# Time-mix and GELU feed-forward layer: the output projection as three float32r passes over truncated operands, and a weight term kept in DRAM

## The chip, the cores and the metric

The kernel runs on one core of one Trainium2 chip. A core has a TensorE (PE, matrix products), a VectorE (DVE), a ScalarE (ACT), a GpSimd (POOL) and a SyncE (SP, which here issues nearly all DMAs), each with its own queue of instructions that it works through in order, and 16 DMA engines. The metric is the device time of one execution in microseconds (us).

## The reference

The input x has 4 sequences of 1024 tokens with 512 channels. It is normalized over the channels, and two branches are added to it: a recurrent time-mix (hidden width 704) and a GELU feed-forward network (hidden width 2048). Cut to what matters:

```python
def _L0_attn_ref(x, ...):
    xx = jnp.concatenate([x[:, 1:2, :], x[:, :-1, :]], axis=1) - x
    k = jnp.einsum('btc,hc->bth', x + xx * time_mix_k, Wk)
    r = jnp.einsum('btc,hc->bth', x + xx * time_mix_r, Wr)
    w = jnp.exp(-jnp.exp(time_decay))
    # for each token t: state = state * w + relu(k_t); out_t = state * r_t
    out = jnp.einsum('bth,ch->btc', out, Wv)
    # layer norm of out over the channels, times ln_gamma, plus ln_beta

def _L0_ffn_ref(x, W0, bias0, W1, bias1):
    X = x.reshape(-1, H).astype(jnp.float16)
    D = jnp.dot(X.astype(jnp.float32), W0.T) + bias0
    D = jax.nn.gelu(D, approximate=False).astype(jnp.float16)
    E = jnp.dot(D.astype(jnp.float32), W1.T) + bias1
    return E.astype(jnp.float16).reshape(B, L, H)

xn = _layernorm(x, axis=-1)
x = x + _L0_attn_ref(xn, ...) + _L0_ffn_ref(xn, ...)
```

The product with Wv is called the output projection below.

## The kernel before

The 4096 tokens are worked through in eight blocks i = 0 to 7 of 512 tokens, two blocks a sequence. Channels and hidden units lie on the 128 partitions: 512 channels are four groups c, the 704 hidden units five groups h of 128 and a half group of 64, and the 2048 units of the feed-forward network 16 chunks n. Output tiles s are 128 tokens by 512 channels, four a block.

**The loop.** A block is 16 iterations, one for each chunk n. In each, TensorE first makes `up` for the chunk two ahead (eight matmuls with the two terms of W0, `w0h` and `w0l`, into the bank `pd`, L659), then `down` for chunk n (eight matmuls that add to four banks `pe`, L681), and then one piece of the time-mix branch. Pieces of chunks 0 to 4 are the five k products of this block, 5 and 6 the half group, 7 to 11 the five r products, and 12 to 15 the output projection of the tiles s = 0 to 3 (in the last block, two at chunk 12 and two at chunk 13). What follows a piece, its evictions above all, is emitted in the next iteration behind the next `up`. The order of TensorE and SP is written out by hand in all blocks; that of VectorE and ScalarE by hand in block 0 alone, and by a scheduler later, which fills in by priority and readiness.

**Arithmetic.** [...]Where a float32 product is wanted in float32r, `three_pass` (L534) splits both operands: u is the operand with its low 12 bits masked away, l the rest. `pa` gathers u and l against the two high terms of the weights (eight matmuls), `pb` a third combination (four matmuls, L335), and ScalarE and VectorE put the two together (L546, L547). The k and r products of blocks 1 to 7 are made in this manner. The output projection is not: `out_full` (L588) multiplies the gated states g by Wv in plain float32 (five matmuls of 128x128 by 512, each shown as two records), and `out_halves` (L600) adds the half group for a pair of tiles with four 64x64 products that lie in the four quadrants of the array.

**What follows the output projection.** `residual` takes the statistics of `po` (L265), normalizes it (L615, L620) and adds it to the residual x (L621). The sum of `pe` is rounded to float16 (`rounded`, L641), added (`finish`, L647) and stored.

**Buffers.** PSUM has eight banks: four for `pe`, four (`ps_mm`) that `pd`, `pa`, `pb`, `ph` and `po` take in turn. A `pd` of the next iteration so takes a bank that an eviction on VectorE or ScalarE has to free. SBUF tiles of 128x512 come from one shared tag q with 53 buffers (`QS`); temporaries have five; w1 has two, kr six. W1 and the split kr weights lie in DRAM as ready-made terms and are loaded for each use; W0's 32 split tiles stay in SBUF.

**The x of the next block** is loaded at chunk 2 (into the same buffer as the residual x, which is loaded at chunk 11), its statistics are taken (L265, L266), POOL makes the reciprocal deviation (L259, L260), VectorE normalizes it (L269) and turns it in 16 transposes (L291). At chunks 11 to 14 it is mixed with its shifted self and split (`mixed`, `split_x`). Block 1 also splits the r weights (`split_kr`) and writes them to DRAM.

Of the kernel before, what the change touches and what calls it, by code (L numbers as in the profile page):

```python
# [22 lines left out]
def time_mix_and_gelu_ffn(  # L23
# [23 lines left out]

    nc = tc.nc  # L50
    B, T, C = x.shape
    HID = wkT.shape[1]
# [3 lines left out]
    NC = C // P  # L56
    NN = N // P
    Q = 32
    QS = 53
    S = 4096.0  # L60
    MASK = -4096

# [19 lines left out]
    def temp(name):  # L82
        return const.tile([P, TB], F32, tag="s", name=name, bufs=5)
# [60 lines left out]
    wv_sb = const.tile([P, NF + 1, C], F32, name="wv_sb")  # L144
    gamma_sb = const.tile([P, C], F32, name="gamma_sb")
    beta_sb = const.tile([P, C], F32, name="beta_sb")
    b1_sb = const.tile([P, C], F32, name="b1_sb")

    def load_late_constants():
        for h in range(NF):  # L150
            nc.sync.dma_start(wv_sb[:, h, :], wvT[h * P : (h + 1) * P, :])
        for half in range(2):
            nc.sync.dma_start(wv_sb[half * HF : (half + 1) * HF, NF, :], wvT[H0:, :])
        nc.sync.dma_start(gamma_sb, gamma.partition_broadcast(P))
        nc.sync.dma_start(beta_sb, beta.partition_broadcast(P))
        nc.sync.dma_start(b1_sb, bias1.partition_broadcast(P))


    def split(hi, lo, raw):
# [1 line left out]
        nc.vector.tensor_sub(lo, raw, hi.bitcast(F32))  # L161

    G = TB // P
    w0 = {}

    w0_raw = {}

# [2 lines left out]
        nc.sync.dma_start(raw, w0T[c * P : (c + 1) * P, g * TB : (g + 1) * TB])  # L170

    def split_w0(g, c):
        w0[c, g] = part(f"w0h_{c}_{g}"), part(f"w0l_{c}_{g}")
        split(*w0[c, g], w0_raw.pop((c, g)))

    w1_dram = [dram.tile([P, 2, C], F32R, name=f"w1d_{n}") for n in range(NN)]
    w1_raw = {}
# [52 lines left out]
    def split_half():  # L230
        u = truncated(raw_half.rearrange("p two c k -> p (two c k)"), "half_u")
        u = u.rearrange("p (two c k) -> p two c k", two=2, c=NC)
        for kind in range(2):
            nc.scalar.copy(half_w[kind][:, :, 0, :], u[:, kind])
            nc.vector.tensor_sub(half_w[kind][:, :, 1, :], raw_half[:, kind], u[:, kind])

    def load_kr(j, kind, h):
        terms = [part(f"kr_{j}_{kind}_{h}_{p}", tag="kr", bufs=6) for p in range(3)]
# [223 lines left out]
            nc.gpsimd.tensor_copy(carry[:hw, h : h + 1], dst[:hw, TB - 1 : TB])  # L462

    def state_tile(j, h):
        gs[j, h] = const.tile([P, TB], F32, tag="g", name=f"g_{j}_{h}", bufs=NF)
        return gs[j, h]

    def gated_half(j, st, r):
        def tokens(ap, odd):
            return ap.rearrange("p (s two t) -> p s two t", two=2, t=P)[:, :, odd, :]  # L470

        ghs[j] = const.tile([P, NS // 2, P], F32, tag="gh", name=f"gh_{j}")
# [18 lines left out]
    def raw_r(j, h):  # L491
        pr = bank(f"pr_{j}_{h}")
        for c in range(NC):
            state["pr"] = product(pr, raw_w[1, h], xrs[j, c], c)

        def after():
            nc.vector.tensor_mul(gs[j, h], gs[j, h], pr)

        return after

# [27 lines left out]
    def three_pass(j, kind, h):  # L528
        xs = xks if kind == 0 else xrs
        w = ks.pop((j, kind, h))  # L530
        pa, pb = bank(f"pa_{j}_{kind}_{h}"), bank(f"pb_{j}_{kind}_{h}")
        for c in range(NC):
            for p in range(2):
                nc.tensor.matmul(  # L534
                    pa,
                    w[p][:, c, :],
                    xs[j, c][p],
                    start=(c == 0 and p == 0),
                    stop=(c == NC - 1 and p == 1),
                )  # L540
        for c in range(NC):
            product(pb, w[2], xs[j, c][2], c)

        def after():
            a, y = temp(f"a_{j}_{kind}_{h}"), temp(f"y_{j}_{kind}_{h}")
            nc.scalar.activation(a, pa, AF.Copy, scale=1.0 + 1.0 / S)  # L546
            nc.vector.scalar_tensor_tensor(y, pb, -1.0 / S, a, ALU.mult, ALU.add)  # L547
            if kind == 0:
                nc.scalar.activation(y, y, AF.Relu)  # L549
                scanned(j, h, P, state_tile(j, h), y)  # L550
            else:
                nc.vector.tensor_mul(gs[j, h], gs[j, h], y)

        return after

# [29 lines left out]
    def out_full(i, s):  # L585
        pos[s] = bank(f"po_{i}_{s}")
        for h in range(NF):
            nc.tensor.matmul(  # L588
                pos[s],
                gs[i, h][:, s * P : (s + 1) * P],  # L590
                wv_sb[:, h, :],
                start=(h == 0),
                stop=False,
            )

    def out_halves(i, pair):
        for s in pair:
            rows = slice(s % 2 * HF, (s % 2 + 1) * HF)
            for t in range(0, P, HF):
                nc.tensor.matmul(  # L600
                    pos[s][t : t + HF],
                    ghs[i][rows, s // 2, t : t + HF],
                    wv_sb[rows, NF, :],
                    start=False,
                    stop=True,
                )

    def residual(i, s):
        po = pos.pop(s)
        mv = small([P, 1, 2], "mv1", f"mvy_{i}_{s}", 4)  # L610
        stats_of(mv, 0, po, f"sty_{i}_{s}")
        rstd = rstd_of(mv[:, :, 1], f"ry_{i}_{s}")
        z = zs[i][:, s, :]
        y = temp(f"o_{i}_{s}")
        nc.vector.scalar_tensor_tensor(  # L615
            y, po, mv[:, 0, 0:1], gamma_sb, ALU.subtract, ALU.mult
        )

        def rest():
            nc.vector.scalar_tensor_tensor(y, y, rstd, beta_sb, ALU.mult, ALU.add)  # L620
            nc.vector.tensor_add(z, z, y)  # L621

        return rest

    def out_piece(i, s):
        out_full(i, s)
        if s % 2 == 0:
            return lambda: None
        pair = (s - 1, s)
        out_halves(i, pair)  # L630

        def after():
            rests = [residual(i, s) for s in pair]
            for rest in rests:
                rest()

        return after
# [16 lines left out]
    def up(i, n):  # L654
        pd = bank(f"pd_{i}_{n}")
        g, k = divmod(n, G)
        for c in range(NC):
            for p in range(2):
                nc.tensor.matmul(  # L659
                    pd,  # L660
                    w0[c, g][p][:, k * P : (k + 1) * P],
                    xf[c],
                    start=(c == 0 and p == 0),
                    stop=(c == NC - 1 and p == 1),
                )
# [76 lines left out]
    for i in range(len(blocks)):  # L742
        with tc.manual_schedule(
# [59 lines left out]
            else:  # L803
# [11 lines left out]
                if j <= LAST:  # L815
# [5 lines left out]
                    put(8, turn, 6, 10)  # L821
                    put(9, turn, 10, 14)
                    put(10, turn, 14, 16)
                mix_at = (11, 12, 13, 14)
            put(11 if j <= LAST else 2, fetch_residual)
            if j <= LAST:
                put(10, x16, j)
# [6 lines left out]
            for n in range(NN):  # L834
                ahead = n + AHEAD
                if ahead == NN and j <= LAST:
                    xf = ffn_input(j)
                nxt = (i, ahead) if ahead < NN else (j, ahead - NN)
                gelu = up(*nxt) if nxt[0] <= LAST else None
                for follow in followers:  # L840
                    follow()
                followers = []
                if gelu:
                    d = gelu()
                if n < NN - tail:
# [80 lines left out]
```

## Time and profile before

| | |
|---|---|
| median of 3 runs | 902.84 us (902.22 to 903.78) |
| profiled execution, whole | 901.21 us |
| profiled execution, span from first to last instruction | 899.4 us |
| TensorE clock granted | 0.996 |
| DMA moved | 165.60 MB, mean 184 GB/s |
| `pe` matmuls (L681) | 1008 records |
| `pd` matmuls (L659) | 1024 records |
| output projection, full groups (L588) | 320 records, 142.2 us busy |
| output projection, half group (L600) | 128 records, 17.4 us busy |
| loads of w1 | 110 of 512 KB, 3.5 us to landing |
| loads of kr | 195 of 256 KB, 4.2 us to landing |
| loads of x | 32 of 256 KB, 5.5 us to landing |

Records of a matmul overlap, so their mean length (0.389 us for float32r, 0.592 us for a float32 record) is longer than the distance at which they follow each other; the chain of waits shows that distance. TensorE's weight loads (PEld) run beside its matmuls. Times in a timeline or a window count from the start of the span.

### The profile page before, as it was taken

How to read it: one execution, taken by the hardware profiler on the slowest of the kernel's cores; microseconds unless marked ns; L12 is line 12 of the kernel's file. 1: busy time of each engine (PE TensorE's matmuls, PEld its weight loads, DVE VectorE, ACT ScalarE, POOL GpSimd, SP SyncE). 2: the span in 40 equal slices, each digit the busy share in tenths (PEclk: the TensorE clock that was granted, in tenths of full speed). 3: DMA queues.
4: the chain of work that ended last, by engine and by line, in shares of the span. 5: the costliest groups of instructions: out<-in, count | busy, mean ns of one | idle time of the engine just before them, and what ended most of it. 6: DMA issues, size and time to landing. Idle time of an engine off the chain costs nothing.

```text
span 899.4 us, 10592 instructions
## 1 busy us (share of the span) xinstructions
PE 886.8 (99%) x3688; PEld 656.7 (73%) x3688; DVE 590.6 (66%) x989; ACT 349.1 (39%) x597; POOL 72.7 (8%) x142
## 2 busy tenths in 40 slices
PE   8999999999999999999999999999999999999996
PEld 8666658876688866888568885788767887588854
DVE  5678885976759558594666955678655776565135
ACT  4855524543234332434323442344323344144320
POOL 1100010100201001000111000010011100000000
PEclk9999999999999999999999999999999999999999
DMA  9569647554285543845448454474535664476621
GB/s 271 210 234 334 225 142 249 183 183 149 101 286 168 177 152 120 291 163 172 139 149 292 146 180 140 160 263 153 173 132 193 226 181 136 141 224 208 192 77 47
DMA packets 77888, 165.60 MB, mean 184 GB/s; under 512 B 9199, under 2 KB 15372, under 8 KB 77836
## 3 DMA queue, kind: packets, MB, share of 16 engines
q1 hardware_dynamic: 77776, 164.92, 55.2%
q8 instruction: 29, 0.48, 0.2%
q14 instruction: 23, 0.19, 0.1%
q10 hardware_dynamic: 60, 0.02, 0.0%
HBM read 140.26 MB, written 24.64 MB: 183 GB/s over the span
## 4 chain that ended last, share of the span: by engine, by line
PE 94%; DVE 4%; issue 1%; DMA 1%; POOL 0%; ACT 0%; SPq 0%; DVEq 0%
PE pd L659 25%; PE pe L681 24%; PE po L588 15%; PE pa L534 13%; PE pb L335 7%; PE ph L562 2%; PE pk L335 2%; PE pr L335 2%; PE po L600 2%; DVE xnT L291 1%; DMA x<-in_L_attn_x 1%; PE idle L353 1%; PE pkr L509 0%; DVE xres L647 0%; DVE stx L265 0%
## 5 line engine op out<-in xcount | busy, mean ns | idle before, releaser
L681 PE MATMUL pe<-w,d 128*128 128x512 f32 x1008 | 249.3, 389 | 0.0
L681 PEld LDWEIGHTS pe<-w,d 128*128 128x128 f32 x1008 | 189.1, 188 | 40.7 <-issue 0.8
L659 PE MATMUL pd<-xf,w0h 128*128 128x512 f32 x512 | 209.3, 409 | 1.4 <-DVE y L547 0.8
L659 PE MATMUL pd<-xf,w0l 128*128 128x512 f32 x512 | 199.7, 390 | 0.0
L669 ACT ACTIVATE d<-pd,late_sb 128x512 f16<-128x512 f32 x128 | 87.7, 685 | 191.7 <-PE pd L659 191.4
L588 PE MATMUL po<-wv_sb,g 128*128 128x512 f32 x320 | 142.2, 592 | 0.0
L547 DVE SCALAR_TENSOR_TENSOR y<-pb,a 128x512 f32<-128x512 f32 x70 | 48.2, 689 | 139.4 <-PE pb L335 124.5
L659 PEld LDWEIGHTS pd<-xf,w0h 128*128 128x128 f32 x512 | 96.1, 188 | 38.9 <-issue 16.5
L659 PEld LDWEIGHTS pd<-xf,w0l 128*128 128x128 f32 x512 | 96.2, 188 | 23.6 <-issue 4.3
L588 PEld LDWEIGHTS po<-wv_sb,g 128*128 128x128 f32 x320 | 60.6, 190 | 64.5 <-issue 62.0
L546 ACT ACTIVATE a<-pa 128x512 f32<-128x512 f32 x70 | 41.8, 597 | 115.0 <-PE pa L534 115.0
L674 ACT CAST d<-d 128x512 fp32r<-128x512 f16 x128 | 79.4, 620 | 3.9
L291 DVE STREAM_TRANSPOSE xnT<-x 32x512 f32<-32x512 f32 x112 | 78.7, 702 | 1.8
L265 DVE BATCH_NORM_STATS2 sty<-po 128x6 f32<-128x512 f32 x32 | 21.9, 684 | 85.9 <-PE po L600 85.9
L534 PE MATMUL pa<-hk,kr 128*128 128x512 f32 x140 | 54.5, 389 | 0.0
L534 PE MATMUL pa<-lk,kr 128*128 128x512 f32 x140 | 54.5, 389 | 0.0
L259 POOL TENSOR_SCALAR ry<-mvy 128x1 f32<-128x1 f32 x32 | 15.2, 476 | 394.6 <-DVE mvy L266 394.6
L534 PE MATMUL pa<-hr,kr 128*128 128x512 f32 x120 | 46.7, 389 | 0.0
L534 PE MATMUL pa<-lr,kr 128*128 128x512 f32 x120 | 46.7, 389 | 0.0
L549 ACT ACTIVATE y<-y 128x512 f32<-128x512 f32 x35 | 22.2, 634 | 61.5 <-DVE y L547 61.5
L246 ACT CAST hk<-uk 128x512 fp32r<-128x512 f32 x28 | 17.4, 620 | 58.3 <-DVE uk L213 58.3
L335 PE MATMUL pb<-mk,kr 128*128 128x512 f32 x140 | 37.4, 389 | 0.0
(133 smaller groups left out, 1039.6 us busy)
## 6 DMA issues: line engine op xcount, KB each, us to landing
w<-w1d SPq DMA_DIRECT2D x110, 512.0 KB, 3.5
kr<-krd SPq DMA_DIRECT2D x195, 256.0 KB, 4.2
x<-in_L_attn_x SPq DMA_DIRECT2D x32, 256.0 KB, 5.5
w1d<-w SPq DMA_DIRECT2D x16, 512.0 KB, 2.9
xres<-in_L_attn_x SPq DMA_DIRECT2D x32, 256.0 KB, 4.6
krd<-wt SPq DMA_DIRECT2D x30, 256.0 KB, 3.6
out<-xres SPq DMA_DIRECT2D x28, 256.0 KB, 4.4
w0raw<-in_L_ffn_W SPq DMA_DIRECT2D x16, 256.0 KB, 5.4
```

The source lines that it names most:

```text
L265: nc.vector.bn_stats(st6, src)
L291: nc.vector.transpose(dst[i * Q : (i + 1) * Q, :, :, j, :], src[j * Q : (j + 1) * Q, :, :, i, :],)
L335: return nc.tensor.matmul(dst, w[:, c, :], src, start=(c == 0), stop=(c == NC - 1))
L534: nc.tensor.matmul(pa, w[p][:, c, :], xs[j, c][p], start=(c == 0 and p == 0), stop=(c == NC - 1 and p == 1),)
L546: nc.scalar.activation(a, pa, AF.Copy, scale=1.0 + 1.0 / S)
L547: nc.vector.scalar_tensor_tensor(y, pb, -1.0 / S, a, ALU.mult, ALU.add)
L549: nc.scalar.activation(y, y, AF.Relu)
L588: nc.tensor.matmul(pos[s], gs[i, h][:, s * P : (s + 1) * P], wv_sb[:, h, :], start=(h == 0), stop=False,)
L659: nc.tensor.matmul(pd, w0[c, g][p][:, k * P : (k + 1) * P], xf[c], start=(c == 0 and p == 0), stop=(c == NC - 1 and p == 1),)
L669: nc.scalar.activation(d16, pd, AF.Gelu, bias=b0_sb[:, n : n + 1])
L674: nc.scalar.copy(d, d16)
L681: nc.tensor.matmul(pe[s] if sum_ is None else sum_, d[:, s * P : (s + 1) * P], w1[p][:, cols], start=(n == first and p == 0), stop=(n == e ...
```

## The change

The output projection of blocks 2 to 7 is made by a new function `out_three_pass`, one tile at a time: 11 float32r matmuls into a bank `oa` and six into a bank `ob`, put together by ScalarE and VectorE, after which `residual` works on the SBUF result in place of PSUM. `gated` splits each g behind its gating multiplication with `split_x` (mask, copy, subtraction, combination), and `gated_half` does so for the half group; its u and l share one tile of 128 partitions, so that `oa` takes them in one matmul over 128 rows, while `ob` takes its combination over 64 rows. Blocks 0 and 1 keep the float32 form. The five and a half groups of Wv are split in block 1 by `split_wv`, at chunks 3, 6, 8, 9, 10 and 11.

To make room, W0's low term leaves SBUF: in block 1 the 16 tiles are written to DRAM (`store_w0l`, four at each of chunks 0, 2, 4 and 6), and from block 2 on a 128x512 tile of it is loaded for each chunk (`load_w0l`), two `up`s ahead, into one of three buffers. Wv and g move to the shared tag q, which has 63 buffers now. In blocks from 2 on the mixing for the next block goes from chunks 11 to 14 to chunks 12 to 15.

```diff
-    QS = 53
+    QS = 63
+    RAW_OUT = 2
...
+    def store_w0l(g):
+        for c in range(NC):
+            terms = w0l[c, g].rearrange("p (n k) -> p n k", k=P)
+            stores.append((w0l_dram[g][:, :, c, :].bitcast(F32), terms.bitcast(F32)))
+
+    def load_w0l(i, n):
+        if i > 1:
+            w0ls[i, n] = part(f"w0l_{i}_{n}", tag="w0l", bufs=3)
+            g, k = divmod(n, G)
+            src = w0l_dram[g][:, k].rearrange("p c k -> p (c k)")
+            nc.sync.dma_start(w0ls[i, n].bitcast(F32), src.bitcast(F32))
...
+    def split_wv(h):
+        raw = wv_raw[h]
+        u = truncated(raw, f"vu_{h}")
+        d = temp(f"vd_{h}")
+        nc.vector.tensor_sub(d, raw, u)
+        if h < NF:
+            wv[h] = [part(f"wv_{h}_{p}") for p in range(3)]
+            nc.scalar.copy(wv[h][0], u)
+            nc.scalar.activation(wv[h][1], d, AF.Copy, scale=S)
+            nc.vector.scalar_tensor_tensor(wv[h][2], d, -S, u, ALU.mult, ALU.add)
+        else:
...
+    def gated(j, h, r):
+        g = gs[j, h]
+        nc.vector.tensor_mul(g, g, r)
+        if j >= RAW_OUT:
+            gs[j, h] = split_x(g, f"g_{j}_{h}")
+
     def gated_half(j, st, r):
+        if j >= RAW_OUT:
+            g = temp(f"gh_{j}")
+            nc.vector.tensor_mul(g[:HF], st[:HF], r)
+            u, l = temp(f"gu_{j}"), temp(f"gl_{j}")
+            nc.vector.tensor_scalar(
+                u[:HF].bitcast(I32), g[:HF].bitcast(I32), MASK, None, ALU.bitwise_and
+            )
+            ghs[j] = part(f"gha_{j}"), part(f"ghb_{j}")
+            nc.scalar.copy(ghs[j][0][:HF], u[:HF])
+            nc.vector.tensor_sub(l[:HF], g[:HF], u[:HF])
+            nc.scalar.copy(ghs[j][0][HF:], l[:HF])
+            nc.vector.scalar_tensor_tensor(
+                ghs[j][1][:HF], l[:HF], -S, u[:HF], ALU.mult, ALU.add
+            )
+            return
...
-        y = temp(f"o_{i}_{s}")
+        y = temp(f"o_{i}_{s}") if i < RAW_OUT else po
...
+    def out_three_pass(i, s):
+        cols = slice(s * P, (s + 1) * P)
+        pa, pb = bank(f"oa_{i}_{s}"), bank(f"ob_{i}_{s}")
+        for h in range(NF):
+            for p in range(2):
+                nc.tensor.matmul(
+                    pa, gs[i, h][p][:, cols], wv[h][p], start=(h == 0 and p == 0), stop=False
+                )
+        nc.tensor.matmul(pa, ghs[i][0][:, cols], wv[NF][0], start=False, stop=True)
+        for h in range(NF):
+            nc.tensor.matmul(pb, gs[i, h][2][:, cols], wv[h][2], start=(h == 0), stop=False)
+        nc.tensor.matmul(
+            pb, ghs[i][1][:HF, cols], wv[NF][1][:HF], start=False, stop=True
+        )
+
+        def after():
+            a, y = temp(f"oa_{i}_{s}"), temp(f"oy_{i}_{s}")
+            nc.scalar.activation(a, pa, AF.Copy, scale=1.0 + 1.0 / S)
+            nc.vector.scalar_tensor_tensor(y, pb, -1.0 / S, a, ALU.mult, ALU.add)
+            residual(i, s, y)()
+
+        return after
...
+        cols = slice(k * P, (k + 1) * P)
+        low = w0ls.pop((i, n)) if i > 1 else None
+        for c in range(NC):
+            wl = w0l[c, g][:, cols] if i < 2 else low[:, c * P : (c + 1) * P]
+            for p, w in enumerate((w0h[c, g][:, cols], wl)):
...
-                mix_at = (11, 12, 13, 14)
+                mix_at = (11, 12, 13, 14) if i < RAW_OUT else (12, 13, 14, 15)
+            if i == 1:
+                for g in range(NN // G):
+                    put(2 * g, store_w0l, g)
+                for h, n in enumerate((3, 6, 8, 9, 10, 11)):
+                    put(n, split_wv, h)
...
+                two_on = (i, ahead + 2) if ahead + 2 < NN else (j, ahead + 2 - NN)
+                if two_on[0] <= LAST:
+                    load_w0l(*two_on)
```

More of the change, by code (lines that the diff above doesn't have):

```diff
@@ L143, in time_mix_and_gelu_ffn @@
     raw_half = part("raw_half", F32).rearrange("p (two c k) -> p two c k", two=2, c=NC)
-    wv_sb = const.tile([P, NF + 1, C], F32, name="wv_sb")
     gamma_sb = const.tile([P, C], F32, name="gamma_sb")
@@ L147, in time_mix_and_gelu_ffn @@
     b1_sb = const.tile([P, C], F32, name="b1_sb")
+    wv_raw, wv = {}, {}
     def load_late_constants():
+        for h in range(NF + 1):
+            wv_raw[h] = part(f"wvraw_{h}", F32)
         for h in range(NF):
-            nc.sync.dma_start(wv_sb[:, h, :], wvT[h * P : (h + 1) * P, :])
+            nc.sync.dma_start(wv_raw[h], wvT[h * P : (h + 1) * P, :])
         for half in range(2):
-            nc.sync.dma_start(wv_sb[half * HF : (half + 1) * HF, NF, :], wvT[H0:, :])
+            nc.sync.dma_start(wv_raw[NF][half * HF : (half + 1) * HF], wvT[H0:, :])
         nc.sync.dma_start(gamma_sb, gamma.partition_broadcast(P))
@@ L163, in time_mix_and_gelu_ffn @@
     G = TB // P
-    w0 = {}
+    w0h, w0l, w0ls = {}, {}, {}
+    w0l_dram = [dram.tile([P, G, NC, P], F32R, name=f"w0d_{g}") for g in range(NN // G)]
     w0_raw = {}
@@ L172, in split_w0 @@
     def split_w0(g, c):
-        w0[c, g] = part(f"w0h_{c}_{g}"), part(f"w0l_{c}_{g}")
-        split(*w0[c, g], w0_raw.pop((c, g)))
+        w0h[c, g], w0l[c, g] = part(f"w0h_{c}_{g}"), part(f"w0l_{c}_{g}")
+        split(w0h[c, g], w0l[c, g], w0_raw.pop((c, g)))
+    def store_w0l(g):
[8 more added lines that the diff above has]
+            nc.sync.dma_start(w0ls[i, n].bitcast(F32), src.bitcast(F32))
     w1_dram = [dram.tile([P, 2, C], F32R, name=f"w1d_{n}") for n in range(NN)]
@@ L235, in split_half @@
             nc.vector.tensor_sub(half_w[kind][:, :, 1, :], raw_half[:, kind], u[:, kind])
+    def split_wv(h):
[9 more added lines that the diff above has]
+        else:
+            wv[h] = [part(f"wv_{h}_{p}") for p in range(2)]
+            nc.scalar.copy(wv[h][0][:HF], u[:HF])
+            nc.scalar.activation(wv[h][0][HF:], d[HF:], AF.Copy, scale=S)
+            nc.vector.scalar_tensor_tensor(
+                wv[h][1][:HF], d[:HF], -S, u[:HF], ALU.mult, ALU.add
+            )
     def load_kr(j, kind, h):
@@ L464, in state_tile @@
     def state_tile(j, h):
-        gs[j, h] = const.tile([P, TB], F32, tag="g", name=f"g_{j}_{h}", bufs=NF)
+        gs[j, h] = part(f"g_{j}_{h}", F32)
         return gs[j, h]
-    def gated_half(j, st, r):
+    def gated(j, h, r):
[3 more added lines that the diff above has]
+            gs[j, h] = split_x(g, f"g_{j}_{h}")
+    def gated_half(j, st, r):
+        if j >= RAW_OUT:
[9 more added lines that the diff above has]
+            nc.scalar.copy(ghs[j][0][HF:], l[:HF])
+            nc.vector.scalar_tensor_tensor(
+                ghs[j][1][:HF], l[:HF], -S, u[:HF], ALU.mult, ALU.add
+            )
+            return
         def tokens(ap, odd):
             return ap.rearrange("p (s two t) -> p s two t", two=2, t=P)[:, :, odd, :]
-        ghs[j] = const.tile([P, NS // 2, P], F32, tag="gh", name=f"gh_{j}")
+        ghs[j] = part(f"gh_{j}", F32)[:, : NS // 2 * P]
+        ghs[j] = ghs[j].rearrange("p (s t) -> p s t", t=P)
         for odd in range(2):
@@ L496, in after @@
         def after():
-            nc.vector.tensor_mul(gs[j, h], gs[j, h], pr)
+            gated(j, h, pr)
         return after
@@ L551, in after @@
             else:
-                nc.vector.tensor_mul(gs[j, h], gs[j, h], y)
+                gated(j, h, y)
         return after
@@ L590, in out_full @@
                 gs[i, h][:, s * P : (s + 1) * P],
-                wv_sb[:, h, :],
+                wv_raw[h],
                 start=(h == 0),
@@ L602, in out_halves @@
                     ghs[i][rows, s // 2, t : t + HF],
-                    wv_sb[rows, NF, :],
+                    wv_raw[NF][rows],
                     start=False,
@@ L606, in out_halves, with residual @@
                 )
-    def residual(i, s):
-        po = pos.pop(s)
+    def residual(i, s, po):
         mv = small([P, 1, 2], "mv1", f"mvy_{i}_{s}", 4)
@@ L623, in residual @@
         return rest
+    def out_three_pass(i, s):
[11 more added lines that the diff above has]
+            pb, ghs[i][1][:HF, cols], wv[NF][1][:HF], start=False, stop=True
+        )
+        def after():
[4 more added lines that the diff above has]
+        return after
     def out_piece(i, s):
+        if i >= RAW_OUT:
+            return out_three_pass(i, s)
         out_full(i, s)
@@ L632, in after @@
         def after():
-            rests = [residual(i, s) for s in pair]
+            rests = [residual(i, s, pos.pop(s)) for s in pair]
             for rest in rests:
@@ L656, in up @@
         g, k = divmod(n, G)
+        cols = slice(k * P, (k + 1) * P)
+        low = w0ls.pop((i, n)) if i > 1 else None
         for c in range(NC):
-            for p in range(2):
+            wl = w0l[c, g][:, cols] if i < 2 else low[:, c * P : (c + 1) * P]
+            for p, w in enumerate((w0h[c, g][:, cols], wl)):
                 nc.tensor.matmul(
                     pd,
-                    w0[c, g][p][:, k * P : (k + 1) * P],
+                    w,
                     xf[c],
```

## The prediction

> **What bounds the kernel now.** I read the page's first two parts first, then the waits of the TensorE, then the chain of waits in one block's output projection, then stage windows, then VectorE's timeline.
>
> ```profile
> PE 886.8 (99%) x3688; PEld 656.7 (73%) x3688; DVE 590.6 (66%) x989; ACT 349.1 (39%) x597; POOL 72.7 (8%) x142
> PEclk9999999999999999999999999999999999999999
> ...
> PE pd L659 <- DVE y L547: 0.8, 1, 0.8
> PE pd L659 <- DVE y L573: 0.6, 1, 0.6
> ...
> 436.40 1.82 PE pe L681 x8
> 438.22 4.29 PE po L588 x10
> 442.51 1.02 PE po L600 x8
> 443.53 2.04 PE pd L659 x8
> 445.57 1.81 PE pe L681 x8
> ...
> 357.73:364.08 6.35, 6.35 (x29) 5.26 (x29) 3.08 (x4) 2.54 (x4) 0.00 (x0) 1.00 0.86 272
> 364.08:370.42 6.34, 6.34 (x29) 5.25 (x29) 3.50 (x5) 2.98 (x5) 0.00 (x0) 1.00 0.87 302
> 370.42:376.77 6.35, 6.35 (x30) 5.26 (x29) 2.31 (x3) 2.54 (x4) 0.00 (x0) 1.00 0.87 296
> ...
> 383.23 1.92 DVE L269 TENSOR_SCALAR x<-x,mvx,rx 128x512 f32<-128x512 f32 x4 [0.29 <-POOL rx L260]
> 399.22 0.68 DVE L573 TENSOR_TENSOR y<-ph,a 64x512 f32<-64x512 f32 x1
> 405.38 0.68 DVE L547 SCALAR_TENSOR_TENSOR y<-pb,a 128x512 f32<-128x512 f32 x1
> ```
>
> TensorE is busy 99% at full clock and waits for data 1.4 us in its own row: its instruction stream is the time. A set of eight float32r matmuls costs 1.81 us (0.227 each), five full float32 ones (ten records, two each) 4.29 us (0.858 each). The windows give busy PE, PEld, DVE, ACT, POOL, then clock, DMA share and GB/s for chunks 0 to 2 of block 3: the DMA engines stand at 0.86 to 0.87 there. The last lines are two PSUM evictions that come close to being late (below).
>
> **What the Trainium skill says.** "TensorEngine Tiling (Array Packing)", Key Properties: a change of tiling mode, not just of tile, drains TensorE. The trace agrees: after 64x64 work the next eight matmuls take 2.04 us instead of 1.81. "TensorE: Matmul & The Clock Gate", Why this matters for your kernels: a single matmul over fewer rows takes as long as over 128. No row of before shows one alone in float32r; I use 0.227 for it. "VectorE: DVE Perf Modes", The TRN2 errata: a float32 tensor_tensor of N columns takes (N+151)/0.96 ns, 691 for 512; the trace has 684 to 691, so new DVE operations of these kinds are priced by existing rows.
>
> **The change part by part.**
>
> *TensorE.* Before, two token tiles cost 4.29 + 4.29 + 1.02, and the switch costs the following sets 0.03 and 0.23: 9.86 us. After, each tile has 10 + 1 matmuls into one bank and 5 + 1 into another: 17 x 0.227 = 3.86, or 7.71 a pair. That would be 2.15 less for each of 12 pairs (blocks 2 to 7): 25.8 us.
> The last of the 17 contracts over 64 rows, so the array goes into a 64x128 tiling and back, once per token tile, 24 times. Price: the old 64x64 set should take 2 x 0.429 = 0.86 if its four quadrants run side by side; it took 1.02, and the set behind it 0.23 too long: 0.39 a round trip. Row tiling alone may be cheaper, and a float32r matmul has the same tail (record 0.389, pitch 0.227: 0.16 to drain on either side). Bounds 0 and 0.5; I take 0.35, 8.4 us in all. Net TensorE gain 25.8 - 8.4 = 17.4 us.
>
> *VectorE, blocks 2 to 6, chunks 3 to 8.* The built order moves the statistics of the next x: before, the fourth aggregate came ahead of the scan and of two splits; after, it stands behind the scan, with only one 0.67 us split between it and the normalization. The chain in before: x arrives (376.43), the aggregate runs at 380.35, POOL's rstd (0.64 + 1.85) ends 2.7 us behind it, and the normalization starts at 383.23, having waited 0.29. After, adding the starts of the reordered items, the aggregate stands 5.8 us behind the arrival instead of 3.9, the normalization 1.9 later, and everything up to the second half eviction (L573) with it. That eviction started at 399.22 and ended 0.68 later; the bank it frees is taken by the pd set that started at 401.25, so about 1.25 us were to spare: 0.6 us late. From there the new half product (0.68 + 0.42 + 0.68 + 0.69 = 2.47 for two gh of 0.42) runs among transposes ahead of the pb eviction (405.38 before, needed for the pd at 407.60): 0.2 us more.
> x can arrive later as well. Chunks 0 to 2 carry 256 KB more each. At 0.87 for 302 GB/s the ceiling is about 350 GB/s (an estimate); three chunks need 290 + 40 = 330. That leaves x late by 0 to 2 us; I take 0.6. In all 0.8 + 0.6 = 1.4 a block, 7 us for five. Bounds 0 and 3.
>
> *VectorE, chunks 7 to 15.* Each of five g gets mask 0.42, subtraction 0.69, combination 0.69: chunk 7 to 11 goes from 1.4 to 3.2 us of the 6.35 (the windows had DVE nearly idle there). Chunks 12 to 15 get an extra eviction of 0.69: mixing 4.0 and residual 3.7 give 7.7 us, about 7.2 by the start-to-start distances of the timeline, against a chunk of 3.63 + 3.86 + 0.35 = 7.8. It just fits: cost nothing, hidden by TensorE; without the switch cost it would be about level. The four e16 that free pe for block j end some 10 us after the third piece, and down needs them at 10.7 to 11.0. ScalarE at 39% has room for the 0.6 us copies.
>
> *Block 1.* Six splits of Wv (mask, subtraction, combination: 1.8 us each, and two ACT copies) go where DVE already stalled PE (both PE waits above are here). The built order puts the first into a 2.6 us idle wait for x and moves four transposes behind the y eviction. Following the two orders side by side, the half eviction comes about 2.3 us late, later ones 1.7 to 2.9. The 16 stores of W0's low terms (256 KB in 512-byte pieces) run in chunks 0 to 6 and crowd x and w1. I take 3 us; bounds 0 and 8.
>
> *SP and W0's low term.* Each chunk issues one 256 KB load behind w1 (0.32 us of issue), 96 in all, 25 MB. It has a buffer of its own (three), so it waits for nothing but its turn; it leaves some 9 us before its up and kr loads of this size land in 4.2. Behind it on SP are kr, x and w1; none gains a wait on compute. Nothing, unless the DMA engines saturate (rival C).
>
> *End.* Before, DVE runs 12.6 us from the last pair's statistics (884.08) to the last add (896.64). After, the third tile's residual runs a piece earlier, and behind the last piece stand one residual with its eviction (0.69 + 0.67 + 0.18 + 0.74 + 0.74 + 0.68 = 3.7), two bases (1.3), the adds of two whole tiles (2.6) and of four half tiles (3.3): 10.9. Gain about 1.5.
>
> **Sum.** Profiled execution 901.2 - 17.4 + 7 + 3 - 1.5 = 892.3. The median of the runs shown stands 1.6 above the profiled execution (902.84 against 901.21), so 894.
>
> **Rivals.**
> A, the forecast: less TensorE work, a drain for every 64-row matmul, DVE lateness in chunk 8. 887 to 900. Chance 0.52.
> B, the plain count: tiling by rows costs next to nothing and the stalls are small. For it: the trace of before has no 64x128 form at full clock, and splitting columns, not rows, may be what cost the 0.39. Against: the page above, which names any change of mode. 901.2 - 25.8 - 1.5 + 2 to 8 = 876 to 882, 877 to 884 as a median: about 881. Chance 0.22.
> C, slower: x lands late because the DMA engines, at 0.87 in chunks 0 to 2 of each block, are pushed to their ceiling. For it: block needs of about 330 GB/s against some 350, and x stands last in that queue. Against: the fill before chunk 0 and after chunk 4 (0.30 share) is low, so the backlog clears. Each us of lateness is a us of stall in blocks 1 to 6. It decides from where six blocks lose 17.4 + 1.5, some 3.2 us a block, so x later by about 2.5. At 4 us: 901.2 - 18.9 + 6 x 4.8 = 911, 913 as a median. Chance 0.16.
> D, no difference: gain and stalls cancel within 1.8 us. Chance 0.10.
>
> **How the numbers follow.** A measurement of this kernel can tell about 0.2% (1.8 us) from no change. A and B are faster: 0.74. D is the same: 0.10. C is slower: 0.16. The predicted time is A's, 894. The range leaves out the fast part of B and most of C: 880 to 904; A's own is 887 to 900.
>
> **What would show it.** Right: the output matmuls in 3.9 to 4.4 us a tile; the pd set behind them over 1.9; PE waits for DVE evictions (half and pb) of about 1 us once a block in blocks 2 to 6 near chunk 8; POOL's rx named for 2 us before the normalization; DVE near 76% of its span (590.6 and about 91 more). Wrong: a pd set of 1.81 behind the 64-row matmul (B), or pd waiting for w0l, or DVE for x by over 4 us (C). The most doubtful steps are the 0.35 and the lateness of x.

## The result, and the profile after

The kernel after takes 891.75 us (median of 4 runs, 891.38 to 892.05) against 902.53 us for the kernel before in the same comparison: ratio 0.9878, 95% interval 0.9861 to 0.9895. Its profiled execution took 891.54 us, with a span of 889.7, 9.7 less than before.

The first part of the page of the kernel after (busy time, share of the span, instructions), then rows of its waits (engine and line, what it waited for, us in total, times, longest):

```profile
PE 874.0 (98%) x3760; PEld 683.6 (77%) x3760; DVE 676.6 (76%) x1133; ACT 389.5 (44%) x675; POOL 75.5 (8%) x142
```

```profile
PEld ob L697 <- issue: 8.4, 24, 0.4
...
PEld pd L748 <- DVE y L635: 6.9, 6, 2.0
PEld pd L748 <- DVE y L609: 5.5, 8, 0.8
PE pd L748 <- DVE y L635: 4.4, 5, 1.6
...
PE pd L748 <- DVE y L609: 1.9, 6, 0.4
```

The line numbers have moved: L748 is the `pd` set, L770 the `pe` set, L635 the half eviction, L609 the pb eviction, L691 to L697 the new output projection. TensorE still sets the time, but now waits for VectorE some 6 us in its own row. The first of these rows names nothing that it waits for: it is the weight load of the 64-row matmul, idle 0.35 us each of 24 times. The chain of waits of the kernel after in block 3 (start, us, what) shows what stands there:

```profile
438.54 2.27 PE oa L691 x10
440.81 0.23 PE oa L694
441.04 1.13 PE ob L696 x5
442.17 0.43 PE ob L697
442.60 2.01 PE pd L748 x8
444.61 1.81 PE pe L770 x8
```

Sixteen matmuls at 0.227 us, then one that takes 0.43, then a `pd` set of 2.01 instead of 1.81: one trip into the 64-row form and back costs 0.40 us beside the matmul itself.

Where the 9.7 us went can be read from the starts of the `pd` sets, one for each chunk. The four output chunks of a block and the one behind them took 7.52 + 9.47 + 7.65 + 9.47 + 6.48 = 40.59 us before and 7.78 + 3 x 7.88 + 6.45 = 37.87 after.

| | predicted, us | measured, us |
|---|---|---|
| output projection, six blocks at 2.72 less | -17.4 | -16.3 |
| stalls in chunks 7 to 9, blocks 2 to 6 | +7 | +8.8 |
| block 1 | +3 | -0.3 |
| end, behind the last output piece | -1.5 | -1.6 |
| start and block 0 | 0 | -0.2 |

The start also differs from one execution to the next: the first `pd` set begins 32.8 us into the span in the two executions compared here, and 33.0 to 34.5 in those of the experiments, none of which changes anything ahead of it. Their spans are therefore read by chunks below.

The stalls are the second row of interest. Chunk 7 is 5.2 us longer over five blocks than before, chunk 8 2.9, chunk 9 0.7. VectorE's timeline of the kernel after in block 4 (start, us, instruction, idle time before it and what ended it), where chunk 3 began at 477.43:

```profile
483.79 0.70 DVE L304 BATCH_NORM_STATS2 stx<-x 128x6 f32<-128x512 f32 x1 [3.47 <-DMA x<-in_L_attn_x]
...
489.29 0.17 DVE L305 BATCH_NORM_AGGREGATE mvx<-stx 128x2 f32<-128x6 f32 x1
...
491.35 1.91 DVE L308 TENSOR_SCALAR x<-x,mvx,rx 128x512 f32<-128x512 f32 x4 [1.25 <-POOL rx L299]
...
507.50 0.68 DVE L635 TENSOR_TENSOR y<-ph,a 64x512 f32<-64x512 f32 x1
...
508.95 0.68 DVE L516 TENSOR_TENSOR gh<-st,y 64x512 f32<-64x512 f32 x1
...
513.02 0.68 DVE L525 SCALAR_TENSOR_TENSOR ghb<-gl,gu 64x512 fp32r<-64x512 f32 x1
...
514.45 0.69 DVE L609 SCALAR_TENSOR_TENSOR y<-pb,a 128x512 f32<-128x512 f32 x1
```

Three distances tell the story: from the start of chunk 3 to the first statistics of x (6.36 here), from there to the second half eviction (23.71), and from that to the pb eviction (6.95). Between the second and the last of these lines only the 1.25 us for POOL is idle: from the arrival of x on, VectorE works through a queue. The `pd` set of chunk 8 is due 29.92 us behind the start of chunk 3, and its bank is free 0.74 us after the half eviction starts, so this one must start by 29.18; the pb eviction, due for chunk 9's `pd` at 36.27, by 35.53. In block 3 of the kernel before, chunk 3 began at 371.17, x arrived with this line, and the two evictions started at 399.22 and 405.38:

```profile
376.43 0.69 DVE L265 BATCH_NORM_STATS2 stx<-x 128x6 f32<-128x512 f32 x1 [2.32 <-DMA x<-in_L_attn_x]
```

The means over blocks 2 to 6, in us:

| | x behind chunk 3 | x to half eviction | half to pb eviction | stalls, chunks 7 / 8 / 9 (sum of five) |
|---|---|---|---|---|
| before | 5.67 | 22.96 | 6.01 | 0.1 / 0.1 / 0.0 |
| after | 6.47 | 23.77 | 6.95 | 5.3 / 3.1 / 0.7 |

So each of three distances grew by 0.8 to 0.95 us, and there were only 0.55 to spare on the mean. x itself lands later in fuller windows. The stage windows of chunks 2 and 3 of block 4 (busy PE, PEld, DVE, ACT, POOL, then clock, DMA share, GB/s), first in the kernel before, then in the kernel after:

```profile
473.40:479.75 6.35, 6.35 (x29) 5.25 (x28) 3.44 (x5) 2.98 (x5) 0.56 (x1) 1.00 0.89 316
479.75:486.10 6.35, 6.35 (x29) 5.26 (x28) 2.16 (x3) 2.54 (x4) 0.19 (x1) 1.00 0.81 268
```

```profile
471.09:477.43 6.34, 6.34 (x29) 5.26 (x28) 3.52 (x5) 2.98 (x5) 0.56 (x1) 1.00 0.99 332
477.43:483.78 6.35, 6.35 (x29) 5.26 (x28) 1.92 (x2) 2.54 (x4) 0.18 (x1) 1.00 0.93 313
```

### The profile page after: what moved, and what is told of

The parts are those of the page before. It is cut to its first block, busy times and chain, and to the rows that moved or that the text cites. A ratio compares the mean times of both kernels' runs of the same rounds, so it can differ in the third digit from the quotient of the medians.

```text
span 889.7 us, 11084 instructions
## 1 busy us (share of the span) xinstructions
PE 874.0 (98%) x3760; PEld 683.6 (77%) x3760; DVE 676.6 (76%) x1133; ACT 389.5 (44%) x675; POOL 75.5 (8%) x142
## 4 chain that ended last, share of the span: by engine, by line
PE 55%; DVE 19%; DMA 3%; issue 2%; POOL 1%; ACT 0%; SPq 0%; DVEq 0%
PE pd L748 15%; PE pe L770 14%; PE pa L596 9%; DVE xnT L330 6%; PE oa L691 6%; PE pb L374 4%; DMA x<-in_L_attn_x 3%; PE ob L696 3%; PE po L650 2%; DVE stx L304 1%; DVE g L492 1%; DVE y L609 1%; PE ob L697 1%; DVE lr L286 1%; DVE y L635 1%
## 5 line engine op out<-in xcount | busy, mean ns | idle before, releaser
L770 PE MATMUL pe<-w,d 128*128 128x512 f32 x1008 | 249.0, 390 | 0.0
L770 PEld LDWEIGHTS pe<-w,d 128*128 128x128 f32 x1008 | 189.2, 188 | 39.6 <-issue 0.2
L748 PE MATMUL pd<-xf,w0h 128*128 128x512 f32 x512 | 207.7, 406 | 6.5 <-DVE y L635 4.4
L748 PE MATMUL pd<-xf,w0l 128*128 128x512 f32 x512 | 199.8, 390 | 0.0
L748 PEld LDWEIGHTS pd<-xf,w0h 128*128 128x128 f32 x512 | 96.1, 188 | 42.3 <-issue 10.3
L609 DVE SCALAR_TENSOR_TENSOR y<-pb,a 128x512 f32<-128x512 f32 x70 | 48.2, 689 | 94.0 <-PE pb L374 83.1
L748 PEld LDWEIGHTS pd<-xf,w0l 128*128 128x128 f32 x512 | 96.3, 188 | 20.6 <-issue 1.9
L691 PE MATMUL oa<-wv,hg 128*128 128x512 f32 x120 | 46.9, 391 | 0.0
L691 PE MATMUL oa<-wv,lg 128*128 128x512 f32 x120 | 46.7, 389 | 0.0
L285 ACT CAST hk<-uk 128x512 fp32r<-128x512 f32 x28 | 17.4, 622 | 47.5 <-DVE uk L234 47.5
L650 PE MATMUL po<-wvraw,g 128*128 128x512 f32 x80 | 35.6, 592 | 0.0
```

Of the source, the lines that this page charges most:

```text
L650: nc.tensor.matmul(pos[s], gs[i, h][:, s * P : (s + 1) * P], wv_raw[h], start=(h == 0), stop=False,)
L691: nc.tensor.matmul(pa, gs[i, h][p][:, cols], wv[h][p], start=(h == 0 and p == 0), stop=False)
L748: nc.tensor.matmul(pd, w, xf[c], start=(c == 0 and p == 0), stop=(c == NC - 1 and p == 1),)
L770: nc.tensor.matmul(pe[s] if sum_ is None else sum_, d[:, s * P : (s + 1) * P], w1[p][:, cols], start=(n == first and p == 0), stop=(n == e ...
```

## The experiments

**The price of the 64-row matmul.** Rows of zeros let the last matmul of `ob` run over all 128 rows.

```diff
+            nc.gpsimd.memset(wv[h][1][HF:].bitcast(F32), 0.0)
...
-            ghs[j] = part(f"gha_{j}"), part(f"ghb_{j}")
+            if not ghb:
+                ghb.append(part("ghb"))
+                nc.gpsimd.memset(ghb[0][HF:].bitcast(F32), 0.0)
+            ghs[j] = part(f"gha_{j}"), ghb[0]
...
-            pb, ghs[i][1][:HF, cols], wv[NF][1][:HF], start=False, stop=True
+            pb, ghs[i][1][:, cols], wv[NF][1], start=False, stop=True
```

> The half group's combination and its weights get 64 rows of zeros each, written once, and the last matmul into ob runs over 128 rows; nothing else is changed. Theory (the change of tiling mode costs 0.41 us a tile, 24 times): the pd set behind it falls from 2.01 to 1.81 us and the piece from 4.06 to 3.86; 9.8 us less than the kernel after, less what VectorE cannot follow in chunks 12 to 15: 881 to 885. Rival (the set is long for another reason, such as the bank it waits for): pd stays at 2.01 and the time at 891 to 892.

Measured: 883.53 us (882.35 to 885.46), ratio to before 0.9796 (0.9783 to 0.9809). The chain of waits of this kernel, same block and columns as above:

```profile
437.54 2.27 PE oa L696 x10
439.81 0.23 PE oa L699
440.04 1.13 PE ob L701 x5
441.17 0.23 PE ob L702
441.40 1.81 PE pd L753 x8
```

The same 17 matmuls, 0.43 down to 0.23 and 2.01 to 1.81, and the output chunks are 7.48 us in place of 7.88. VectorE, busy 6.7 to 7.2 us in such a chunk of block 4, keeps up. The stalls of chunks 7 to 9 stay (8.5 us in all). That the change of form, and not the bank, costs the time is shown.

The opposite check leaves that matmul out altogether.

```diff
-            nc.tensor.matmul(pb, gs[i, h][2][:, cols], wv[h][2], start=(h == 0), stop=False)
-        nc.tensor.matmul(
-            pb, ghs[i][1][:HF, cols], wv[NF][1][:HF], start=False, stop=True
-        )
+            nc.tensor.matmul(
+                pb, gs[i, h][2][:, cols], wv[h][2], start=(h == 0), stop=(h == NF - 1)
+            )
```

> The last matmul into ob, over 64 rows, is left out, and with it the half group's third term; everything else is as in the kernel after. Theory (what the change of mode costs is 0.41 us beside the 0.227 of the matmul): each of the 24 tiles is shorter by 0.64, chunks 12 to 15 take 7.26 us, and the time falls by 14 to 15.5 us to 876 to 878. Rival (VectorE, busy 6.9 us in each of these chunks, sets their length once TensorE needs less than about 7.5): chunks of 7.4 to 7.5 and 881 to 883.

Measured: 879.23 us (878.83 to 880.88), ratio 0.9749 (0.9736 to 0.9762). The output chunks took 7.25 us as the theory has it, so VectorE does not set them. The time lies between the two forecasts for other reasons, as far as the profiled execution shows them (880.88 us, the slowest of the four): the stalls of chunks 7 to 9 were 10.5 us instead of 9.0, 3.7 of them in block 5, where the half eviction came 24.55 us behind an x that was itself late (6.62); the first `pd` set began 1.4 us later; and from chunk 3 of block 7 to the end only 1.5 us were gained, where four tiles at 0.63 would give 2.5.

**When x arrives.** At chunk 2, x is issued ahead of kr.

```diff
+                    if k == 4 and j <= LAST:
+                        put(2, fetch_x)
                     if k > 1:
                         put(k - 2 + 2 * (k > 6), fetch_kr, i, kind, h)
...
-                    put(2, fetch_x)
```

> At chunk 2 the load of the next x is issued ahead of the kr loads instead of behind them. Theory (the stalls of 8.7 us in chunks 7 to 9 come from a VectorE chain that begins with the arrival of x): x lands 1.5 to 2.7 us earlier, the half eviction with it, the stalls fall to 0 to 3 us, and the time to 884 to 887. Rival 1 (the new work behind the half eviction is what stalls, whenever x comes): 891 to 892. Rival 2 (kr is late now, and the k product waits for it): PE waits for kr, 892 to 900.

Measured: 884.59 us (883.37 to 885.44), ratio 0.9805 (0.9792 to 0.9817). In block 4, whose chunk 3 starts at 476.04, SP's timeline now has

```profile
474.85 1.75 SPq L105 DMA_DIRECT2D x<-in_L_attn_x  x4
476.70 1.91 SPq L279 DMA_DIRECT2D kr<-krd  x3
```

while x's issue came 0.57 us behind that start in the kernel after. The statistics of x begin 4.32 us behind it on the mean, 2.15 earlier; the half eviction follows 24.40 behind x, 0.6 more than without the edit; the stalls of chunks 7 to 9 are 1.5 us in place of 9.0. Nothing waits for kr. So the lateness is one chain that begins with x, as the first theory has it.

**What makes x late.** Four loads of W0's low term around x's are left out.

```diff
-        if i > 1:
+        if i > 1 and n in (3, 4, 5, 6):
+            w0ls[i, n] = w0ls[i, n - 1]
+        elif i > 1:
```

> From block 2 on, the four loads of W0's low term that lie around the load of x (for the chunks 3 to 6) are left out and the tile of the chunk before them is used again, so that the feed-forward output of these chunks lacks its right low term; the number of matmuls is the same. Theory (these transfers make x late by the 0.8 us that the kernels before and after differ in, on the mean of blocks 2 to 6): x's statistics start 5.5 to 5.8 us behind the chunk's boundary again instead of 6.5, the stall in chunk 7 falls by 0.6 to 0.8 us a block, chunk 8 keeps its 0.6, and the time is 887 to 889. Rival (x is late for SP's issue or another reason, or the order of the statistics alone makes the stall): 891 to 892.

Measured: 890.84 us (889.07 to 892.47), ratio 0.9874 (0.9861 to 0.9887), not told apart from the kernel after. The first half of the theory holds: x's statistics begin 5.70 us behind the boundary, as before the change (5.67). Of the second half, some holds: chunk 7 stalls 3.3 us in five blocks instead of 5.3, where 3 to 4 us less were forecast. The profiled execution as a whole does not show these 2.0 us: its first `pd` set began 1.4 us later, and block 1, which the edit leaves as it is, took 0.8 us more behind an x that came 6.49 us behind the boundary instead of 5.70. VectorE's timeline in block 4 of this kernel, chunk 3 starting at 478.32:

```profile
484.97 0.69 DVE L306 BATCH_NORM_STATS2 stx<-x 128x6 f32<-128x512 f32 x1 [3.76 <-DMA x<-in_L_attn_x]
...
490.54 0.55 DVE L310 TENSOR_SCALAR x<-x,mvx,rx 128x512 f32<-128x512 f32 x1 [1.48 <-POOL rx L301]
...
509.02 0.68 DVE L637 TENSOR_TENSOR y<-ph,a 64x512 f32<-64x512 f32 x1
```

The scheduler has reordered the queue as well: the normalization starts 5.57 us behind x instead of 7.56, yet the half eviction comes 24.05 behind it instead of 23.71. The normalization's place does not matter; the work and the idle time in front of the eviction do, and the wait for POOL grew from 1.25 to 1.48. So the half eviction gains 0.4 us on the mean where x gains 0.8. Blocks also differ by chance: x came 5.08 to 6.65 behind.

**The order of the statistics.**

```diff
-                    put(4, stats, *range(NS))
+                    put(3, stats, *range(NS))
```

> The statistics of the next x get their priority at chunk 3 instead of 4, which puts the fourth aggregate ahead of the scan again, as in the kernel before. Theory (the order of the aggregate and the scan delays the normalization by some 0.8 to 1.9 us a block): the stall in chunk 7 falls by 0.8 us in each of five blocks, the time to 885 to 889. Rival (only the arrival of x counts): the time stays at 891 to 892. If the statistics block VectorE while x is on its way, slower: 893 to 897.

Measured: 890.45 us (889.91 to 891.75), ratio 0.9873 (0.986 to 0.9885): not told apart from the kernel after. In four of five blocks the half eviction came 23.3 to 23.5 us behind x, 0.35 less than after, with the wait for POOL at 0.94; the fifth took 24.5, with 1.06 us of idle time for a later part of x. In this profiled execution chunk 7 stalls 2.7 us instead of 5.3, but three quarters of that come from an x that arrived 0.4 us earlier, which the edit does not touch. The theory overstated it: the order is worth 0.35 us a block in four blocks and 0.13 on the mean.

**The memory half of the change alone.** All blocks project in float32.

```diff
-    RAW_OUT = 2
+    RAW_OUT = 8
```

> All eight blocks keep the output projection in plain float32; the splits of Wv and W0's low term in DRAM with its load for every chunk stay. This is the memory half of the change alone. Theory: W0's low term costs no wait of its own but makes x late by about 1 us, and the scheduler's order delays the normalization, so chunk 7 stalls by 0.8 us in five blocks, and without the new half product chunk 8 does not: 905 to 908. Rival 1 (the loads are free and all stalls come from the new half product): as before, 902 to 903. Rival 2 (the loads cost more than the pieces after show, hidden by the shorter output pieces): 910 or more.

Measured: 907.02 us (906.17 to 909.27), ratio 1.0059 (1.0047 to 1.0071). Its waits:

```profile
PEld pd L748 <- DVE y L635: 5.7, 6, 1.5
PE pd L748 <- DVE y L635: 3.1, 6, 1.1
```

So W0's low term in DRAM and the order that comes with it cost 5 us by themselves: x 6.15 us behind the boundary, the half eviction 23.78 behind x as in the kernel after, and 3.8 us of stall in chunk 7. But the pb eviction follows 6.01 behind the half eviction, as before the change, and chunk 8 stalls 0.7 us in all instead of 3.1. The two halves of the stall are thus parted: chunk 7's is that of x and the order, chunk 8's is that of the new half product (gh, gu, gl, ghb). No `pd` waited for the tile of W0 itself.

**Is VectorE's queue what holds the half eviction?** Ten transposes are left out from block 2 on.

```diff
-                    put(6, turn, 0, 2)
-                    put(7, turn, 2, 6)
-                    put(8, turn, 6, 10)
+                    if i < RAW_OUT:
+                        put(6, turn, 0, 2)
+                        put(7, turn, 2, 6)
+                        put(8, turn, 6, 10)
```

> The kernel after without 10 of the 16 transposes of the next x from block 2 on (the transposed x keeps old values there, so blocks 3 to 7 are computed from partly old input); everything else is left as it is, and VectorE's order has 6 transposes ahead of the second half eviction where it had 10, and none between it and the pb eviction where it had 5 to 6. Theory (from the arrival of x on VectorE is simply full, and the eviction is late by the work that stands in front of it): the second half eviction starts 20.7 to 21.1 us behind x's statistics instead of 23.7 to 23.9, and all 8.7 us of stall in chunks 7 to 9 of blocks 2 to 6 go: 882 to 884. Rival 1 (the eviction waits for TensorE or ScalarE, whatever VectorE has to do): 891 to 892. Rival 2 (only the half product's own chain is late, in chunk 8): 887 to 889.

Measured: 886.9 us (886.49 to 888.48), ratio 0.983 (0.9816 to 0.9843), none of the forecasts' mechanisms alone. VectorE's and ScalarE's timelines of this kernel in block 4, chunk 3 starting at 476.86 and x's statistics at 483.00:

```profile
503.25 0.71 DVE L330 STREAM_TRANSPOSE xnT<-x 32x512 f32<-32x512 f32 x1
506.30 0.68 DVE L635 TENSOR_TENSOR y<-ph,a 64x512 f32<-64x512 f32 x1 [2.33 <-ACT a L634]
```

```profile
504.00 1.66 ACT L343 CAST x<-xnT 128x512 f16<-128x512 f32 x3 [1.45 <-DVE xnT L330]
505.68 0.58 ACT L634 COPY a<-ph 64x512 f32<-64x512 f32 x1
```

VectorE was free at 503.97, 20.97 us behind x, as the theory has it. But with fewer transposes the float16 copies of x are ready sooner, the order has three of them ahead of the eviction's first half on ScalarE, and they wait for the last transpose. The half eviction so waits 2.33 us for ScalarE and comes at 23.3, and chunk 7 stalls 3.3 us. In chunk 8, where the transposes between the two evictions are gone, these lie 3.88 us apart and 0.7 us of stall is left. The queue is confirmed for chunk 8; in chunk 7 the edit moved a second queue, so it does not settle the matter there. That an eviction is late by what stands ahead of it on its engines is all that it shows.

**Block 1.** The first split of Wv is moved from chunk 3 to chunk 7.

```diff
-                for h, n in enumerate((3, 6, 8, 9, 10, 11)):
+                for h, n in enumerate((7, 6, 8, 9, 10, 11)):
```

> The kernel after with one change: the first split of Wv goes from chunk 3 of block 1 to chunk 7, so that it no longer lies in VectorE's wait for x but between the two half evictions. Theory (this wait is what hid it, and the prediction's 3 us for block 1 fell away for such reasons): the second half eviction comes 1.8 us later than 29.3 behind the boundary, block 1 is 1.5 to 1.8 us longer than 110.5, the time 893 to 894. Rival (other idle time of VectorE takes it up): block 1 at 110.5 to 110.8, the time 891.5 to 892.

Measured: 892.66 us (891.54 to 894.24), ratio 0.9897 (0.9881 to 0.9913). The expectation misplaced the split: it came to lie behind the second half eviction, which kept its place, 29.17 us behind chunk 3 (29.31 in the kernel after). Block 1 took 111.0 us, 0.5 more. That alone would show little, since runs that leave block 1 as it is take 110.45 to 111.3 by when x comes. But its chunks 8 to 11 take 27.1 to 27.2 us in all of those, and 27.8 here: 0.6 more. Two thirds of the split's 1.8 us were absorbed. So the wait for x hides some of it, not the 1.5 us or more that I expected.

**Both helpful edits together**, with zeros and x first:

> The two edits that helped alone, in one kernel: 64 rows of zeros for the last matmul into ob, and x loaded ahead of kr. They act in different chunks (12 to 15, and 2 to 9), so theory: their gains add, 8.2 and 7.2 us off the 891.75 of the kernel after, 875 to 878. Rival (the shorter chunks 12 to 15 bring the transfers of the next block closer together, or VectorE is full there): 879 to 883.

Measured: 875.9 us (875.41 to 877.05), ratio 0.9712 (0.9699 to 0.9726). The gains add: output chunks of 7.48 us, stalls of 0.4 us in chunks 7 to 9.

**Block 1 in three passes too**, on top of these:

```diff
-    RAW_OUT = 2
+    RAW_OUT = 1
```

> The kernel with both edits, and block 1 in three passes too, so that only block 0 is in plain float32; block 1 now splits Wv and g in the same chunks. TensorE needs 34.1 - 30.0 = 4.1 us less in block 1's chunks 12 to 15. Theory (VectorE already makes TensorE wait about 2 us in block 1's chunks 7 to 11, and gets 10 us more there): 2 to 4 us of the gain are lost again, 0 to 2 us less than the kernel with both edits, 874 to 877. Rival (the new work fits between the evictions): 871 to 873. If the splits make chunk 12 wait for wv, slower than the kernel with both edits: 878 to 882.

Measured: 873.31 us (873.21 to 875.17), ratio 0.9685 (0.9672 to 0.9698), 2.6 us less, between theory and rival. In its profiled execution TensorE's 4.1 us are there, block 1's stalls in chunks 7 to 11 grow by 1.9 us (3.6 for 1.7), and chunk 12 is 1.1 too long; the splits of Wv and g do take back most of the gain.

Then the splits of Wv go ahead of x:

```diff
-                for h, n in enumerate((3, 6, 8, 9, 10, 11)):
+                for h, n in enumerate((0, 1, 1, 2, 2, 3)):
```

> The kernel in three passes from block 1 on, with the six splits of Wv at chunks 0, 1, 1, 2, 2 and 3 of block 1 instead of 3, 6, 8, 9, 10 and 11. Theory (VectorE has no room from the arrival of x to the last pb eviction, but idles for 3 us a chunk before it; so the half eviction lies a fixed 23 to 24 us behind x's arrival, plus the work put between): with five splits of 1.8 us ahead of x, the stalls of block 1's chunks 8 to 12, 4.6 us, fall to 0.5 to 2, and the time to 869.5 to 872. Rival (the stalls there come from splitting g, or from evictions waiting for TensorE): 873 to 874. Should the splits run into the pb evictions of chunks 0 to 2, slower: 875 or more.

Measured: 872.79 us (871.77 to 874.9), ratio 0.968 (0.9664 to 0.9697), not told apart. The stalls of chunks 7 to 11 did fall, from 3.6 to 0.9 us. But chunk 4 became 8.47 us long. TensorE's and ScalarE's timelines there:

```profile
168.38 0.50 PE L753 MATMUL pd<-xf,w0h 128*128 128x512 f32 x1 [1.97 <-ACT a L613]
```

```profile
166.45 0.62 ACT L271 CAST wv<-vu 64x512 fp32r<-64x512 f32 x1 [2.60 <-PE pb L375]
167.08 0.63 ACT L272 ACTIVATE wv<-vd 64x512 fp32r<-64x512 f32 x1
167.73 0.60 ACT L613 ACTIVATE a<-pa 128x512 f32<-128x512 f32 x1
```

ScalarE's copy of the last split waits 2.60 us for TensorE's pb matmuls. The copy reads no result of theirs, so I read this as a wait for a buffer of the shared tag; the eviction `a`, which a `pd` needs, stands behind it. Two of the splits later:

```diff
-                for h, n in enumerate((0, 1, 1, 2, 2, 3)):
+                for h, n in enumerate((0, 1, 2, 3, 6, 8)):
```

> As the kernel with the early splits, but at chunks 0, 1, 2, 3, 6 and 8 of block 1 in place of 0, 1, 1, 2, 2 and 3. Theory (the 2.0 us for which TensorE waited in chunk 4 came from ScalarE, whose copies of the last split stood in front of the eviction a and waited for a buffer of the shared tag that the k product's matmuls still read): with two splits later this wait is gone, and 1.5 to 2.5 us of the stalls in chunks 7 to 12 come back; 871 to 873. Rival (another wait for a buffer takes its place): 873 to 875.

Measured: 872.45 us (870.38 to 874.13), ratio 0.9666 (0.9651 to 0.9682). The wait in chunk 4 is gone, and the stalls in chunks 7 to 11 are 2.6 us instead of 0.9. That the wait was one for a buffer fits this but is not shown: the edit also took the last split's copies out of chunk 4's way. The last three kernels can't be told apart; each is some 19 us faster than the kernel after.

## Why the prediction was right or wrong

The forecast, A, is what happened: 894 forecast, 891.75 measured; against the profiled execution 892.3 and 891.5. The sum was met partly by cancelling: TensorE gained 1.1 us less than forecast and the stalls were 1.8 longer, and block 1 gave 3.3 back. So the mechanism was right, and that the sum came within 1 us of the profiled execution was in part luck.

*TensorE.* The count of 17 matmuls at 0.227 us was right. The drain was the doubtful step, 0.35 taken from a different form (64x64); it is 0.40, by the 7.88 and 7.48 us of the chunks with and without it. Rival B, where row tiling costs nothing, is excluded. The prediction's net gain of 17.4 us was 16.3.

*VectorE, chunk 7.* The mechanism was right, the half eviction late for the bank of chunk 8's `pd`, but a part of its working was not. The fourth aggregate did move behind the scan: in block 4 it starts 5.50 us behind x where it had started 3.92 behind. The prediction took the normalization and all behind it to be 1.9 us later for this, with a wait for POOL of 2 us. The normalization came 0.8 later (7.56 behind x for 6.74) and the wait grew from 0.29 to no more than 1.25, because POOL's second operation, which lies between aggregate and normalization, took less. Here it is in the kernel before and then in the kernel after:

```profile
490.76 1.80 POOL L260 TENSOR_TENSOR rx<-rx,nhalf 128x4 f32<-128x4 f32 x1
```

```profile
490.27 1.04 POOL L299 TENSOR_TENSOR rx<-rx,nhalf 128x4 f32<-128x4 f32 x1
```

With 1.80 us again the wait would have been 2.0 (an estimate from these figures); why it took less stays open. What delays the half eviction is this idle time and not the place of the normalization: the queue between x and the eviction holds the same work wherever it stands, and the run with fewer loads of W0's term moved the normalization by 2 us while the eviction came no sooner behind x. With the statistics at chunk 3 the wait was 0.94 and the eviction 0.35 sooner. The half eviction moved 0.8 behind x on the mean, 1.07 in blocks 3 to 6; in block 2 VectorE had waited 1.09 us for a later part of x before the change. The 1.25 us to spare were read in block 3 alone, which had the most of the five; their mean was 0.55. x came 0.8 us later, not 0.6, in this execution; in the seven profiled executions that have all these loads and the same order of issue it came 6.1 to 6.5 us behind the boundary on the mean, 0.4 to 0.8 later, so the 0.6 was a fair price. The errors cancelled: 0.6 + 0.6 us a block forecast, 1.05 measured.

*VectorE, chunk 8.* The new half product among transposes was priced at 0.2 us. This is the step that failed by most in blocks 2 to 6: it cost 0.6 a block in chunk 8 and 0.1 in chunk 9. The two evictions are 0.95 us further apart, and the first was already late, so nothing was there to hide it: from then on the second has one chunk of 6.35 us behind the first, in which 6.01 us fit and 6.95 are 0.60 too long. The run with float32 everywhere shows 0.1 in its place.

*Chunks 12 to 15.* "It just fits" was right, with more room than thought: chunks went down to 7.25 us without VectorE making TensorE wait.

*Two readings of the lines.* The prediction's three windows begin 0.7 us ahead of chunks 1, 2 and 3 of block 3, going by the starts of its `pd` sets (358.47, 364.82, 371.17), and not with chunks 0 to 2; chunk 0 had a DMA share of 0.22. And VectorE was nearly idle only in chunks 9 and 10 there, 1.39 us busy in each, while chunks 7 and 8 had 6.19 and 5.56. Neither moved the sum: the loads do meet a full stage, and the splits of g came in chunks 9 to 11 (5.06, 4.59 and 3.19 us busy after the change).

*Block 1.* The largest error: +3 us forecast, -0.3 measured. The step that failed is the half eviction "about 2.3 us late". It starts 29.31 us behind chunk 3 where it had started at 29.90: the order has five transposes ahead of it instead of eight (2.1 us less), which pays for the one split that lies between x and it (1.8 us), and x was not late there (5.70 against 5.81 us). I had the moved transposes in hand, but did not take them off this eviction. The run that moved the first split shows that its place is worth 0.6 us.

*SP and W0's term.* No direct wait worth naming, as forecast (one weight load waited 0.2 us for a tile of it); the indirect cost is x's delay, shown by leaving four loads out. Rival C has the right mechanism, DMA at 0.93 to 0.99 in these windows, at a fifth of the 4 us it priced.

*End.* 1.6 us, forecast 1.5.

*The page on tiling.* What the Trainium skill states under "TensorEngine Tiling (Array Packing)", Key Properties, that a change of tiling mode drains TensorE, decided between A and B. It holds for row tiling too: 0.40 us a trip.

## What to carry to other kernels

A matmul over fewer rows between full ones paid 0.40 us for the change of form each time; rows of zeros, written once, cost nothing on TensorE and took 8.2 us off. Where one engine works through a fixed queue from the arrival of a transfer to an eviction that TensorE needs, price a change by the work and idle time between these two, in every block and not in the best one, and move the transfer ahead in its queue before reordering the work: x ahead of kr was worth 7.2 us, the order of the statistics nothing that the time shows. When work is taken off one engine's queue, look at what now comes first on the engine that feeds it.

## What the runs showed that I had not expected

- A float32r matmul of 64x128 by 512 among full ones takes 0.43 us to the next and makes the following set of eight 2.01 instead of 1.81; over 128 rows, 64 of them zero, 0.23 and 1.81.
- The DMA share of a window reached 0.99 at 332 GB/s with loads of 256 and 512 KB, and x was still only 0.8 us later on the mean.
- POOL's second operation on 128x4 elements took 1.80 to 1.86 us in blocks 1 to 6 of the kernel before and 1.04 in those of the kernel after, and VectorE's start behind it agrees with both.
